# Cross attention on one core: x1 and x2 stored by halves of n, and the first batch's keys and scores made in two halves of m

## Chip, cores and metric

The kernel runs on one core of a Trainium2 chip. The metric is the device time of one execution in microseconds, given as the median of several runs. The kernel before takes 717.22 us (three runs, 717.07 to 717.47).

## What is computed

```python
# B, C1, C2, N = 8, 512, 512, 1024; D = 64; float32
q = jnp.einsum('bcn,dc->bnd', x1, Wq) + bq
k = jnp.einsum('bcn,dc->bdn', x2, Wk) + bk[:, None]
v = jnp.einsum('bcn,dc->bdn', x2, Wv) + bv[:, None]
attn = jax.nn.softmax(jnp.einsum('bnd,bdm->bnm', q, k), axis=2)
attn_out = jnp.einsum('bcm,bnm->bcn', v, attn)
return attn_out + x1
```

For each of eight batches, x1 (512 channels by 1024 positions n) gives queries and x2 (512 by 1024 positions m) gives keys and values. The softmax runs over m.

## The kernel before, in words

Everything is float32. The kernel never forms v: it computes y = x2 times the exponentials, transposed, divides by their sum, and then takes Wv times y, plus bv, plus x1. Both of these products are cut into 2 by 2 blocks and done with seven block products instead of eight; sums of blocks on the left (`left_sums`, L91: S1 to S4) and on the right (`right_sums`, L233: T1 to T4) are made by DVE (VectorE). `MULT` (L259) lists the seven products with their operands and the PSUM banks, "a" or "c", that collect them. In the text "product 6" is entry 6 of this table. `first(i)` (L435) is one of the products with x2, `second(i)` (L438) one of those with Wv.

**A batch** has two halves of n, h = 0 and 1, of 512. The scores are laid with m on the partitions: eight blocks of 128 values of m, by 512 of n. `scores` (L164) makes a pair of such blocks, i of 0 to 3, g of 0 and 1: two matmuls, one on the upper and one on the lower 64 rows of TensorE (PE). In the kernel before, pair i holds m block i (g = 0) and block 4 + i (g = 1), and lies in the tile `e[h]` at `[:, :, i, :]`. `fold` (L194) takes the running maximum (later the sum) over pairs on DVE, `highest` (L207) folds the two g and lets POOL (GpSimd) reduce over partitions to `top`. `exponentials` (L227) subtracts `top` on DVE and takes exp on ACT (ScalarE). `total` and `shares` do the same for the sums and their reciprocals.

**Projections.** `project` (L130) makes q or k of a whole batch: for each of four channel blocks c, one matmul of 64 columns for n below 512 into PSUM partitions 0 to 63 and one for n from 512 into partitions 64 to 127, each with 512 columns to stream. `load_x` (L111) loads x1 or x2 of a batch in four transfers of 512 KB, one per channel block, into one tile `x` that has a single buffer: x2 of a batch is issued when the queries have read x1 of it, and x1 of the next batch when the keys have read x2.

**Order.** The order of each engine's instructions is the order in which the program issues them (`manual_schedule`); a framework adds the waits. Each engine takes its instructions strictly in that order. Loads and stores are issued from one queue, SP's; ACT's queue issues the weights wqk and a copy of q's halves to the other partitions (L156). When ACT copies a score pair that DVE also reads from PSUM, it waits for DVE's reading.

**The head** (L349) is batch 0 up to its first product. SP issues, in this order: x1 for h = 0 in two transfers of two channel blocks each (rows of 2 KB), x2 in four transfers (rows of 4 KB), a11 (a transposed block of x2), x1 for h = 1 in two, a21, a22, a12, and the four blocks of Wv. PE does ten warm-up matmuls, then q of h = 0 on both partition halves (`head_queries`, L339, bank c1), k of all m (bank c0), four score pairs (two in the double-buffered "sc" banks, one in a0 and a1, one in c0 and c1), q of h = 1 in bank a0, three score pairs of h = 1, and then `first(1)`, the first product, whose right operand is the exponentials of g = 0. ACT copies the score pairs to SBUF in the order 0, 2, 3, 1. DVE folds pair 1 from PSUM and pairs 2 and 3 from the copies, and makes S1 and S2 of batch 0 while POOL reduces the maximum.

**`head_second`** (L408) follows in period 0 (`period`, L431), after `first(1)`: the fourth score pair of h = 1, the queries of batch 1, the second half's maximum, S3 and S4 of batch 0, and the exponentials of h = 1. Then come `sum_e(T1, T2)`, which makes the right operand of product 6, and, on PE, `first(2)`, the keys of batch 1 and `first(6)`.

**The end of period 0.** DVE adds bias and x1 to what the banks hold (`evict_o`, L319): the results 11, 22, 12 and 21 in this order. Before 12, it makes S1 to S4 of batch 1 (L529). Result 12 is in bank a, which `first(1)` of batch 1 opens anew. Each eviction issues its stores on SP; `fetch_o` (L312) loads x1 again for it.

The order of the first copies and folds is set in these lines (L386 to L392):

```python
        copies = [scores(s, 0, i, bank) for i, bank in enumerate((None, None, "a", "c"))]
        copies[0]()
        fold(s, 0, 1, "max", ALU.max, copies[1].ps)
        for i in (2, 3, 1):
            copies[i]()
        fold(s, 0, 2, "max", ALU.max)
        fold(s, 0, 3, "max", ALU.max)
```

Of the kernel before, what the change touches and what calls it, by code (L numbers as in the profile page):

```python
# [15 lines left out]
def kernel(  # L16
# [39 lines left out]

    nc = tc.nc
    P = 128
    B, C, N = x1.shape
    D = wqk.shape[3]  # L60
    CT = C // P
    H = 512
# [41 lines left out]
    class Batch:  # L104
        def __init__(self, b):
# [2 lines left out]
            self.mx, self.top, self.den, self.rden = {}, {}, {}, {}  # L108
            self.tmp, self.bank = {}, {}

    def load_x(s, x):  # L111

        s.x = sb.tile([P, CT, N], F32, tag="x", name=f"x_{s.b}_{x.tensor.name}")
        for c in range(CT):
            nc.sync.dma_start(s.x[:, c, :], x[s.b, ts(c, P), :])

    def load_a(s, *ks):
        for k in ks:
# [8 lines left out]
                s.a[k] = sb.tile([P, MH, C // 2], F32, tag=f"a{k}", name=f"a{k}_{s.b}")  # L127
        left_sums(s.a, *ks)

    def project(s, nm, w_sb, bank=None):  # L130

        if bank:
            ps = ps_a.tile([P, H], F32, tag=bank, name=f"ps_{nm}_{s.b}")
        else:
            ps = ps_s.tile([P, 2, H], F32, tag="sc", name=f"ps_{nm}_{s.b}")[:, 0, :]
        for c in range(CT):
            for h, r in ((0, lo), (1, hi)):
                nc.tensor.matmul(  # L138
                    ps[r, :],
                    w_sb[:, c, :],  # L140
                    s.x[:, c, ts(h, H)],
                    start=(c == 0),
                    stop=(c == CT - 1),
                )
        return ps
# [9 lines left out]
        for h, r, o in ((0, lo, hi), (1, hi, lo)):  # L155
            nc.scalar.dma_start(s.q[o, ts(h, H)], s.q[r, ts(h, H)])  # L156

    def keys(s, bank=None):

        ps = project(s, "k", wk_sb, bank)  # L160
        s.k = sb.tile([P, H], F32, tag="k", name=f"k_{s.b}", bufs=2)
        nc.scalar.activation(s.k, ps, AF.Identity, bias=bk_sb)

    def scores(s, h, i, bank=None):  # L164


        if i == 0:
            s.e[h] = sb.tile([P, 2, MH, H], F32, tag=f"e{h}", name=f"e_{s.b}_{h}")
        e = s.e[h]
        if bank:  # L170
            whole = None
            ps = [
                ps_a.tile([P, H], F32, tag=f"{bank}{g}", name=f"ps_s{bank}{g}_{s.b}_{h}_{i}")
                for g in range(2)
            ]
        else:
            whole = ps_s.tile([P, 2, H], F32, tag="sc", name=f"ps_s_{s.b}_{h}_{i}")
            ps = [whole[:, g, :] for g in range(2)]
        for g, r in ((0, lo), (1, hi)):
            nc.tensor.matmul(  # L180
                ps[g], s.k[r, ts(i, P)], s.q[r, ts(h, H)], start=True, stop=True
            )

        def copy():
            if bank:
                for g in range(2):
                    nc.scalar.copy(e[:, g, i, :], ps[g])  # L187
            else:
                nc.scalar.copy(e[:, :, i, :], whole)  # L189

        copy.ps = whole
        return copy

    def fold(s, h, i, kind, op, ps=None):  # L194

        e = s.e[h]
        if i == 1:
            s.mx[h] = sb.tile([P, 2, H], F32, tag="fold", name=f"{kind}_{s.b}_{h}", bufs=2)
        f = s.mx[h]
        new = e[:, :, i, :] if ps is None else ps  # L200
        nc.vector.tensor_tensor(f, e[:, :, 0, :] if i == 1 else f, new, op)  # L201

    def fold_halves(s, h, op):
        f = s.mx[h]
# [20 lines left out]
        nc.scalar.activation(e, e, AF.Exp)  # L225

    def exponentials(s, h, i):  # L227
        e = s.e[h][:, :, i, :]
        top = s.top[h].unsqueeze(1).to_broadcast([P, 2, H])
        nc.vector.tensor_tensor(e, e, top, ALU.subtract)  # L230
        nc.scalar.activation(e, e, AF.Exp)  # L231
# [80 lines left out]
    def fetch_o(s, k):  # L312

        for j in range(2):
            c, h = 2 * (int(k[0]) - 1) + j, int(k[1]) - 1
            s.o[k, j] = sb.tile([P, H], F32, tag="o", name=f"o{k}{j}_{s.b}", bufs=6)
            nc.sync.dma_start(s.o[k, j], x1[s.b, ts(c, P), ts(h, H)])

    def evict_o(s, k):  # L319
        bank, add = RESULT[k]  # L320
# [18 lines left out]
    def head_queries(s, x_sb, h, bank):  # L339

        ps = ps_a.tile([P, H], F32, tag=bank, name=f"ps_q_{s.b}_{h}")
        for c in range(CT):
            for r in (lo, hi):
                nc.tensor.matmul(
                    ps[r, :], wq_sb[:, c, :], x_sb[:, c, ts(h, H)], start=(c == 0), stop=(c == CT - 1)
                )
        nc.scalar.activation(s.q[:, ts(h, H)], ps, AF.Identity, bias=bq_sb)  # L347

    def head(s):  # L349

        s.q = sb.tile([P, N], F32, tag="q", name=f"q_{s.b}", bufs=2)
        x1_sb = sb.tile([P, CT, N], F32, tag="x", name="x1_head")
        x2_sb = sb.tile([P, 2, MH, H], F32, tag="e1", name="x2_head")
        s.x = x2_sb.rearrange("p a (b t) n -> p (a b) (t n)", t=2)

        def load_x1(c, h):  # L360
            nc.sync.dma_start(
                x1_sb[:, c : c + 2, ts(h, H)],
                x1[s.b, c * P : (c + 2) * P, ts(h, H)].rearrange("(t p) n -> p t n", p=P),
            )

        nc.gpsimd.dma_start(bqk_sb, bqk)
        nc.gpsimd.dma_start(bv_sb, bv)
        nc.scalar.dma_start(wqk_sb, wqk)
        warm = const.tile([P, P], F32, name="warm")
        nc.vector.memset(warm, 0.0)  # L370
        ps = ps_a.tile([P, H], F32, tag="a0", name="ps_warm")
        for _ in range(WARM):
            nc.tensor.matmul(ps[:, 0:P], warm, warm, start=True, stop=True)
        load_x1(0, 0)
        load_x1(2, 0)
        for c in range(CT):
            nc.sync.dma_start(s.x[:, c, :], x2[s.b, ts(c, P), :])
        nc.scalar.activation(warm[:, 0:1], warm[:, 0:1], AF.Exp)
        load_a(s, "11")
        load_x1(0, 1)  # L380
        load_x1(2, 1)
        load_a(s, "21", "22", "12")
        load_values()
        head_queries(s, x1_sb, 0, "c1")
        keys(s, "c0")
        copies = [scores(s, 0, i, bank) for i, bank in enumerate((None, None, "a", "c"))]  # L386
        copies[0]()
        fold(s, 0, 1, "max", ALU.max, copies[1].ps)
        for i in (2, 3, 1):
            copies[i]()  # L390
        fold(s, 0, 2, "max", ALU.max)
        fold(s, 0, 3, "max", ALU.max)  # L392
        highest(s, 0)
        sum_a(s, "S1", "S2")
        head_queries(s, x1_sb, 1, "a0")
        load_x(states[1], x1)
        copies = [scores(s, 1, 0), scores(s, 1, 1), scores(s, 1, 2, "c")]
        for g in range(2):
            for i in range(MH):
                first_exponentials(s, g, i)  # L400
        for copy in copies:
            copy()
        fold(s, 0, 1, "sum", ALU.add)
        fold(s, 0, 2, "sum", ALU.add)
        fold(s, 1, 1, "max", ALU.max)
        fold(s, 0, 3, "sum", ALU.add)

    def head_second(s, n):  # L408
# [5 lines left out]
        queries(n)  # L414
        load_x(n, x2)
        highest(s, 1)
        sum_a(s, "S3", "S4")
        for i in range(MH):
            exponentials(s, 1, i)

# [10 lines left out]
    def period(s, n, nn, nnn):  # L431
# [94 lines left out]
        second(7)  # L526
        evict_o(s, "22")
        if s.b == 0:
            sum_a(n, "S1", "S2", "S3", "S4")  # L529
        if n:  # L530
            second(3)
            evict_o(s, "12")
            second(4)
            evict_o(s, "21")
        else:
            second(4)
            evict_o(s, "21")
# [39 lines left out]
```

## Time and profile before

| | |
|---|---|
| median of the runs | 717.22 us |
| the profiled execution's own time | 716.93 us |
| its span, first to last instruction | 714.9 us |
| PE busy | 705.6 us (99%), 1892 instructions |
| weight loads (PEld) busy | 299.8 us (42%) |
| DVE busy | 590.2 us (83%), 569 instructions |
| ACT busy | 201.3 us (28%) |
| POOL busy | 97.2 us (14%) |
| DMA | 87.39 MB, mean 122 GB/s |
| granted TensorE clock | 1.000 of full speed |

Busy time is the time in which an engine executes instructions, waiting left out; the 2.0 us between the execution's own time and its span lie before the first and after the last instruction. A line of the timeline gives start and duration in us, engine, source line, operation, output and inputs by the names of their tiles, sizes and the number of instructions that it merges. What stands in brackets is how long the engine was idle ahead of it, and what released it. Matmuls are pipelined, so that a row's duration reaches some tenths beyond the start of the next. One float32 matmul of the program is two rows of the profile. The tile names `ps_ya` and `ps_yc` are the banks a and c in the products with x2, `ps_oa` and `ps_oc` those with Wv, `ps_s`, `ps_sa`, `ps_sc` are scores in the "sc", a and c banks, `aS` and `a` are blocks of x2 and their sums, `eT` the sums of exponentials.

### The profile page before, as it was taken

Reading aid. Unit: us, or ns where it says so; the run is one execution under the profiler, and the core shown is the slowest. Engines: PE = TensorE matmul, PEld = TensorE weight load, DVE = VectorE, ACT = ScalarE, POOL = GpSimd, SP = SyncE. Lnnn points to the kernel's source line nnn. Section 1 sums busy time; section 2 is a strip of 40 time slices with the busy share of each in tenths; the row PEclk is TensorE's granted clock in tenths of the full one; section 3 lists DMA queues with packets and bytes.
Section 4 is the critical chain, followed back from the end, with each engine's and each line's share of the span. In section 5 each row is a group of like instructions: output and inputs, shape, how many; then the busy total and the mean of one; then the engine's idle time right before and its main releaser. Section 6 shows DMA issues by size and latency. Waiting matters only on the chain.

```text
span 714.9 us, 5407 instructions
## 1 busy us (share of the span) xinstructions
PE 705.6 (99%) x1892; PEld 299.8 (42%) x1892; DVE 590.2 (83%) x569; ACT 201.3 (28%) x271; POOL 97.2 (14%) x38
## 2 busy tenths in 40 slices
PE   8999999999999999999999999999999999999997
PEld 4333444434444434444344444443434444444443
DVE  0999899988979888798887987889887898989454
ACT  2733412043211522224231232403324034220010
POOL 0132030030200211021200202002020020301000
PEclk9999999999999999999999999999999999999999
DMA  8577132441333503435133252232601350042004
GB/s 333 210 235 256 68 147 101 156 154 46 147 146 119 189 8 141 148 118 191 58 119 127 109 191 98 108 118 89 220 0 61 117 177 0 0 161 75 0 1 147
DMA packets 34699, 87.39 MB, mean 122 GB/s; under 512 B 3952, under 2 KB 3952, under 8 KB 34672
## 3 DMA queue, kind: packets, MB, share of 16 engines
q1 hardware_dynamic: 33344, 84.95, 33.6%
q10 hardware_dynamic: 1264, 2.10, 0.9%
q8 instruction: 15, 0.25, 0.1%
q14 instruction: 12, 0.10, 0.0%
q0 software_dynamic: 64, 0.00, 0.0%
HBM read 68.42 MB, written 16.78 MB: 119 GB/s over the span
## 4 chain that ended last, share of the span: by engine, by line
PE 87%; DVE 8%; DMA 1%; issue 1%; ACT 1%; SPq 0%; POOL 0%; DVEq 0%; ACTq 0%; POOLq 0%
PE ps_ya L279 27%; PE ps_yc L279 21%; PE ps_oa L279 15%; PE ps_oc L279 11%; PE ps_s L180 5%; PE ps_k L138 3%; PE ps_q L138 3%; DVE max L201 1%; DMA x_head<-in_x_dram 1%; DVE eT L236 1%; DVE e L230 1%; DVE aS L100 1%; PE ps_sa L180 1%; DVE den L219 1%; PE ps_sc L180 1%
## 5 line engine op out<-in xcount | busy, mean ns | idle before, releaser
L215 POOL PARTITION_ALL_REDUCE den<-sum x16 | 65.3, 4081 | 433.2 <-DVE sum L205 433.2
L279 PE MATMUL ps_ya<-eT,aS 128*128 128x512 f32 x256 | 113.1, 595 | 0.0
L279 PE MATMUL ps_yc<-e,a 128*128 128x512 f32 x256 | 112.6, 592 | 0.0
L289 ACT COPY uy<-ps_ya 128x512 f32<-128x512 f32 x48 | 28.1, 588 | 233.2 <-PE ps_ya L279 233.2
L230 DVE TENSOR_TENSOR e<-e,top 128x1024 f32<-128x1024 f32 x60 | 70.0, 1219 | 13.9 <-POOL top L210 13.9
L279 PEld LDWEIGHTS ps_ya<-eT,aS 128*128 128x128 f32 x256 | 48.0, 190 | 63.8 <-issue 63.6
L279 PEld LDWEIGHTS ps_yc<-e,a 128*128 128x128 f32 x256 | 48.6, 190 | 61.6 <-issue 60.1
L324 DVE SCALAR_TENSOR_TENSOR o<-ps_oc,bv_sb,o 128x512 f32<-128x512 f32 x48 | 35.7, 749 | 41.6 <-PE ps_oc L279 41.5
L231 ACT ACTIVATE e<-e 128x1024 f32<-128x1024 f32 x60 | 62.2, 1056 | 22.2 <-DVE e L230 20.4
L289 ACT COPY uo<-ps_oa 128x512 f32<-128x512 f32 x48 | 28.1, 586 | 132.4 <-PE ps_oa L279 131.1
L189 ACT COPY e<-ps_s 128x1024 f32<-128x1024 f32 x47 | 46.7, 1027 | 61.5 <-PE ps_s L180 61.5
L279 PE MATMUL ps_ya<-e,a 128*128 128x512 f32 x128 | 56.4, 594 | 1.3 <-ACT e L225 0.8
L279 PE MATMUL ps_oc<-y,w 128*128 128x512 f32 x128 | 57.5, 592 | 0.0
L279 PE MATMUL ps_oa<-yT,w_S 128*128 128x512 f32 x128 | 57.5, 592 | 0.0
L279 PE MATMUL ps_yc<-eT,a 128*128 128x512 f32 x128 | 57.0, 598 | 0.0
L279 PE MATMUL ps_ya<-e,aS 128*128 128x512 f32 x128 | 56.2, 592 | 0.0
L219 DVE RECIPROCAL den<-den 128x512 f32<-128x512 f32 x16 | 53.6, 3349 | 0.0
L180 PE MATMUL ps_s<-q,k 64*128 64x512 f32 x188 | 47.9, 608 | 1.6 <-ACT q L347 0.8
L210 POOL PARTITION_ALL_REDUCE top<-max x16 | 30.3, 1897 | 131.3 <-DVE max L205 131.3
L308 DVE TENSOR_TENSOR y<-ps_yc,uy 128x512 f32<-128x512 f32 x48 | 31.2, 676 | 15.0 <-PE ps_yc L279 14.9
L201 DVE TENSOR_TENSOR max<-max,e 128x1024 f32<-128x1024 f32 x32 | 39.2, 1225 | 3.7 <-ACT e L187 0.5
L201 DVE TENSOR_TENSOR sum<-sum,e 128x1024 f32<-128x1024 f32 x32 | 39.2, 1225 | 2.1
(65 smaller groups left out, 757.5 us busy)
## 6 DMA issues: line engine op xcount, KB each, us to landing
x_in_x_dram<-in_x_dram SPq DMA_DIRECT2D x56, 512.0 KB, 5.4
a<-in_x2T_dram SPq DMA_DIRECT2D x32, 512.0 KB, 4.2
o<-in_x_dram SPq DMA_DIRECT2D x64, 256.0 KB, 6.4
out_dram<-o SPq DMA_DIRECT2D x64, 256.0 KB, 2.1
x_head<-in_x_dram SPq DMA_DIRECT2D x8, 512.0 KB, 8.0
q<-q ACTq DMA_DIRECT2D x14, 128.0 KB, 6.9
w<-in_wvT_dram SPq DMA_DIRECT2D x4, 256.0 KB, 8.9
wqk_sb<-in_wqk_dram ACTq DMA_DIRECT2D x1, 256.0 KB, 4.7
```

The source lines that it names most:

```text
L138: nc.tensor.matmul(ps[r, :], w_sb[:, c, :], s.x[:, c, ts(h, H)], start=(c == 0), stop=(c == CT - 1),)
L180: nc.tensor.matmul(ps[g], s.k[r, ts(i, P)], s.q[r, ts(h, H)], start=True, stop=True)
L189: nc.scalar.copy(e[:, :, i, :], whole)
L201: nc.vector.tensor_tensor(f, e[:, :, 0, :] if i == 1 else f, new, op)
L215: nc.gpsimd.partition_all_reduce(s.den[h], s.mx[h][:, 0, :], P, ReduceOp.add)
L219: nc.vector.reciprocal(s.rden[h], s.den[h])
L230: nc.vector.tensor_tensor(e, e, top, ALU.subtract)
L231: nc.scalar.activation(e, e, AF.Exp)
L279: nc.tensor.matmul(ps, left[ka][:, k, ts(j, P)], right[kb][:, k, :], start=opens and k == 0, stop=i in (2, 3, 4) and k == n_k - 1, skip_gr ...
L289: nc.scalar.copy(s.tmp[i, j], ps)
L308: nc.vector.tensor_tensor(y[:, j, :], ps, s.tmp[add, j], ALU.add)
L324: nc.vector.scalar_tensor_tensor(o, s.bank[bank, j], bv_sb[:, c : c + 1], o, ALU.add, ALU.add)
```

## The change

The arrays x1 and x2 are stored in another order ahead of the launch: [batch, half of n, partition, channel block, 512], so that the values of one partition for one half lie together, two channel blocks in one row of 4 KB. All loads of x follow: `load_x` still has four transfers of 512 KB, but each holds two channel blocks of one half of n, in the order (c 0 and 1, h 0), (c 0 and 1, h 1), (c 2 and 3, h 0), (c 2 and 3, h 1).

In the head, SP issues x1 of h = 0, then x2 of the first half of m, then x2 of the second half, two transfers each; the rest stays in order. A new function `head_keys` projects half of the keys with matmuls of 256 columns: the first quarter of that half into partitions 0 to 63 and the second into 64 to 127. Pairs 0 and 1 now hold blocks of the first half of m, pairs 2 and 3 of the second; `pair` finds their places in `e[h]` for batch 0. PE's order in the head becomes: q of h = 0, first half of k (bank c0), pairs 0 and 1, second half of k (bank a0), pair 2 (c0, c1), pair 3 (a0, a1), q of h = 1 (bank c0). DVE folds pairs 2 and 3 from PSUM as well, in two instructions each, and each copy by ACT comes after the fold of its pair, in the order 0, 1, 2, 3, with the second half's k between copies 0 and 1.

S2 of batch 0 moves from the head to `head_second`, ahead of S3 and S4. S3 and S4 of batch 1 move from before `evict_o(12)` to after `evict_o(21)`.

```diff
@@ -56,7 +56,7 @@
 
     nc = tc.nc
     P = 128
-    B, C, N = x1.shape
+    B, C, N = out.shape
     D = wqk.shape[3]
     CT = C // P
     H = 512
@@ -108,11 +108,18 @@
             self.mx, self.top, self.den, self.rden = {}, {}, {}, {}
             self.tmp, self.bank = {}, {}
 
+        def pair(self, h, i):
+
+            if self.b:
+                return self.e[h][:, :, i, :]
+            return self.e[h][:, i // 2, i % 2 :: 2, :]
+
     def load_x(s, x):
 
-        s.x = sb.tile([P, CT, N], F32, tag="x", name=f"x_{s.b}_{x.tensor.name}")
-        for c in range(CT):
-            nc.sync.dma_start(s.x[:, c, :], x[s.b, ts(c, P), :])
+        s.x = sb.tile([P, 2, CT, H], F32, tag="x", name=f"x_{s.b}_{x.tensor.name}")
+        for c in range(0, CT, 2):
+            for h in range(2):
+                nc.sync.dma_start(s.x[:, h, c : c + 2, :], x[s.b, h, :, c : c + 2, :])
 
     def load_a(s, *ks):
         for k in ks:
@@ -127,18 +134,15 @@
                 s.a[k] = sb.tile([P, MH, C // 2], F32, tag=f"a{k}", name=f"a{k}_{s.b}")
         left_sums(s.a, *ks)
 
-    def project(s, nm, w_sb, bank=None):
-
-        if bank:
-            ps = ps_a.tile([P, H], F32, tag=bank, name=f"ps_{nm}_{s.b}")
-        else:
-            ps = ps_s.tile([P, 2, H], F32, tag="sc", name=f"ps_{nm}_{s.b}")[:, 0, :]
+    def project(s, nm, w_sb):
+
+        ps = ps_s.tile([P, 2, H], F32, tag="sc", name=f"ps_{nm}_{s.b}")[:, 0, :]
         for c in range(CT):
             for h, r in ((0, lo), (1, hi)):
                 nc.tensor.matmul(
                     ps[r, :],
                     w_sb[:, c, :],
-                    s.x[:, c, ts(h, H)],
+                    s.x[:, h, c, :],
                     start=(c == 0),
                     stop=(c == CT - 1),
                 )
@@ -155,9 +159,9 @@
         for h, r, o in ((0, lo, hi), (1, hi, lo)):
             nc.scalar.dma_start(s.q[o, ts(h, H)], s.q[r, ts(h, H)])
 
-    def keys(s, bank=None):
-
-        ps = project(s, "k", wk_sb, bank)
+    def keys(s):
+
+        ps = project(s, "k", wk_sb)
         s.k = sb.tile([P, H], F32, tag="k", name=f"k_{s.b}", bufs=2)
         nc.scalar.activation(s.k, ps, AF.Identity, bias=bk_sb)
 
@@ -166,9 +170,8 @@
 
         if i == 0:
             s.e[h] = sb.tile([P, 2, MH, H], F32, tag=f"e{h}", name=f"e_{s.b}_{h}")
-        e = s.e[h]
+        e = s.pair(h, i)
         if bank:
-            whole = None
             ps = [
                 ps_a.tile([P, H], F32, tag=f"{bank}{g}", name=f"ps_s{bank}{g}_{s.b}_{h}_{i}")
                 for g in range(2)
@@ -184,21 +187,24 @@
         def copy():
             if bank:
                 for g in range(2):
-                    nc.scalar.copy(e[:, g, i, :], ps[g])
+                    nc.scalar.copy(e[:, g, :], ps[g])
             else:
-                nc.scalar.copy(e[:, :, i, :], whole)
-
-        copy.ps = whole
+                nc.scalar.copy(e, whole)
+
+        copy.ps = ps if bank else whole
         return copy
 
     def fold(s, h, i, kind, op, ps=None):
 
-        e = s.e[h]
         if i == 1:
             s.mx[h] = sb.tile([P, 2, H], F32, tag="fold", name=f"{kind}_{s.b}_{h}", bufs=2)
         f = s.mx[h]
-        new = e[:, :, i, :] if ps is None else ps
-        nc.vector.tensor_tensor(f, e[:, :, 0, :] if i == 1 else f, new, op)
+        if isinstance(ps, list):
+            for g in range(2):
+                nc.vector.tensor_tensor(f[:, g, :], f[:, g, :], ps[g], op)
+        else:
+            new = s.pair(h, i) if ps is None else ps
+            nc.vector.tensor_tensor(f, s.pair(h, 0) if i == 1 else f, new, op)
 
     def fold_halves(s, h, op):
         f = s.mx[h]
@@ -225,7 +231,7 @@
         nc.scalar.activation(e, e, AF.Exp)
 
     def exponentials(s, h, i):
-        e = s.e[h][:, :, i, :]
+        e = s.pair(h, i)
         top = s.top[h].unsqueeze(1).to_broadcast([P, 2, H])
         nc.vector.tensor_tensor(e, e, top, ALU.subtract)
         nc.scalar.activation(e, e, AF.Exp)
@@ -314,7 +320,7 @@
         for j in range(2):
             c, h = 2 * (int(k[0]) - 1) + j, int(k[1]) - 1
             s.o[k, j] = sb.tile([P, H], F32, tag="o", name=f"o{k}{j}_{s.b}", bufs=6)
-            nc.sync.dma_start(s.o[k, j], x1[s.b, ts(c, P), ts(h, H)])
+            nc.sync.dma_start(s.o[k, j], x1[s.b, h, :, c, :])
 
     def evict_o(s, k):
         bank, add = RESULT[k]
@@ -342,26 +348,39 @@
         for c in range(CT):
             for r in (lo, hi):
                 nc.tensor.matmul(
-                    ps[r, :], wq_sb[:, c, :], x_sb[:, c, ts(h, H)], start=(c == 0), stop=(c == CT - 1)
+                    ps[r, :], wq_sb[:, c, :], x_sb[:, h, c, :], start=(c == 0), stop=(c == CT - 1)
                 )
         nc.scalar.activation(s.q[:, ts(h, H)], ps, AF.Identity, bias=bq_sb)
 
+    def head_keys(s, x_sb, h, bank):
+
+        ps = ps_a.tile([P, H // 2], F32, tag=bank, name=f"ps_k_{s.b}_{h}")
+        for c in range(CT):
+            for g, r in ((0, lo), (1, hi)):
+                nc.tensor.matmul(
+                    ps[r, :],
+                    wk_sb[:, c, :],
+                    x_sb[:, h, c, ts(g, H // 2)],
+                    start=(c == 0),
+                    stop=(c == CT - 1),
+                )
+        nc.scalar.activation(s.k[:, ts(h, H // 2)], ps, AF.Identity, bias=bk_sb)
+
     def head(s):
 
 
 
 
 
+
         s.q = sb.tile([P, N], F32, tag="q", name=f"q_{s.b}", bufs=2)
-        x1_sb = sb.tile([P, CT, N], F32, tag="x", name="x1_head")
+        s.k = sb.tile([P, H], F32, tag="k", name=f"k_{s.b}", bufs=2)
+        x1_sb = sb.tile([P, 2, CT, H], F32, tag="x", name="x1_head")
         x2_sb = sb.tile([P, 2, MH, H], F32, tag="e1", name="x2_head")
-        s.x = x2_sb.rearrange("p a (b t) n -> p (a b) (t n)", t=2)
-
-        def load_x1(c, h):
-            nc.sync.dma_start(
-                x1_sb[:, c : c + 2, ts(h, H)],
-                x1[s.b, c * P : (c + 2) * P, ts(h, H)].rearrange("(t p) n -> p t n", p=P),
-            )
+
+        def load(x_sb, x, h):
+            for c in range(0, CT, 2):
+                nc.sync.dma_start(x_sb[:, h, c : c + 2, :], x[s.b, h, :, c : c + 2, :])
 
         nc.gpsimd.dma_start(bqk_sb, bqk)
         nc.gpsimd.dma_start(bv_sb, bv)
@@ -371,28 +390,26 @@
         ps = ps_a.tile([P, H], F32, tag="a0", name="ps_warm")
         for _ in range(WARM):
             nc.tensor.matmul(ps[:, 0:P], warm, warm, start=True, stop=True)
-        load_x1(0, 0)
-        load_x1(2, 0)
-        for c in range(CT):
-            nc.sync.dma_start(s.x[:, c, :], x2[s.b, ts(c, P), :])
+        load(x1_sb, x1, 0)
+        load(x2_sb, x2, 0)
+        load(x2_sb, x2, 1)
         nc.scalar.activation(warm[:, 0:1], warm[:, 0:1], AF.Exp)
         load_a(s, "11")
-        load_x1(0, 1)
-        load_x1(2, 1)
+        load(x1_sb, x1, 1)
         load_a(s, "21", "22", "12")
         load_values()
         head_queries(s, x1_sb, 0, "c1")
-        keys(s, "c0")
-        copies = [scores(s, 0, i, bank) for i, bank in enumerate((None, None, "a", "c"))]
+        head_keys(s, x2_sb, 0, "c0")
+        copies = [scores(s, 0, 0), scores(s, 0, 1)]
         copies[0]()
-        fold(s, 0, 1, "max", ALU.max, copies[1].ps)
-        for i in (2, 3, 1):
+        head_keys(s, x2_sb, 1, "a0")
+        copies += [scores(s, 0, 2, "c"), scores(s, 0, 3, "a")]
+        for i in range(1, MH):
+            fold(s, 0, i, "max", ALU.max, copies[i].ps)
             copies[i]()
-        fold(s, 0, 2, "max", ALU.max)
-        fold(s, 0, 3, "max", ALU.max)
         highest(s, 0)
-        sum_a(s, "S1", "S2")
-        head_queries(s, x1_sb, 1, "a0")
+        sum_a(s, "S1")
+        head_queries(s, x1_sb, 1, "c0")
         load_x(states[1], x1)
         copies = [scores(s, 1, 0), scores(s, 1, 1), scores(s, 1, 2, "c")]
         for g in range(2):
@@ -414,7 +431,7 @@
         queries(n)
         load_x(n, x2)
         highest(s, 1)
-        sum_a(s, "S3", "S4")
+        sum_a(s, "S2", "S3", "S4")
         for i in range(MH):
             exponentials(s, 1, i)
 
@@ -526,12 +543,14 @@
         second(7)
         evict_o(s, "22")
         if s.b == 0:
-            sum_a(n, "S1", "S2", "S3", "S4")
+            sum_a(n, "S1", "S2")
         if n:
             second(3)
             evict_o(s, "12")
             second(4)
             evict_o(s, "21")
+            if s.b == 0:
+                sum_a(n, "S3", "S4")
         else:
             second(4)
             evict_o(s, "21")
@@ -555,8 +574,8 @@
     from concourse.bass_utils import run_bass_kernel_spmd as _run
 
     laid = {
-        "x1": _np.asarray(x),
-        "x2": _np.asarray(ctx_2048),
+        "x1": _np.asarray(x).reshape(8, 4, 128, 2, 512).transpose(0, 3, 2, 1, 4),
+        "x2": _np.asarray(ctx_2048).reshape(8, 4, 128, 2, 512).transpose(0, 3, 2, 1, 4),
         "x2T": _np.asarray(ctx_2048).reshape(8, 2, 256, 2, 4, 128).transpose(0, 1, 3, 5, 4, 2),
         "wqk": _np.stack([_np.asarray(L0_xattn_Wq), _np.asarray(L0_xattn_Wk)]).reshape(2, 64, 4, 128).transpose(3, 0, 2, 1),
         "bqk": _np.stack([_np.asarray(L0_xattn_bq), _np.asarray(L0_xattn_bk)] * 2).reshape(2, 2, 64).transpose(0, 2, 1).reshape(128, 2),
```

## The prediction, made before the result was known

> **What bounds the kernel now.** First the busy table by stretches: it tells where TensorE (PE) is not busy at all. Columns: stretch, its length, then busy us (count) of PE, weight loads, DVE, ACT, POOL, clock, DMA share, GB/s.
>
> ```profile
> 6.00:14.36 8.36, 7.35 (x32) 2.29 (x33) 0.00 (x0) 1.37 (x2) 0.00 (x0) 1.00 1.03 401
> 14.36:26.12 11.76, 10.14 (x45) 3.60 (x45) 8.83 (x9) 5.36 (x9) 2.68 (x1) 1.00 0.98 365
> 26.12:50.00 23.88, 23.88 (x71) 8.91 (x72) 23.52 (x24) 15.16 (x21) 2.69 (x1) 1.00 0.49 161
> 50.00:126.00 76.00, 75.30 (x204) 31.40 (x203) 71.52 (x71) 24.09 (x31) 15.08 (x5) 1.00 0.43 155
> 126.00:700.00 574.00, 574.00 (x1500) 245.00 (x1499) 479.47 (x458) 153.25 (x206) 75.19 (x25) 1.00 0.30 106
> ```
>
> From 126 us on PE never stops; before, it loses time only in the head (to 26.12) and twice in batch 0. The change can act there alone, plus whatever it adds to PE later. The list of PE's waits names the two late ones, in place of which the timeline of PE has these rows (start, duration):
>
> ```profile
> 1.04 4.41 PE L373 MATMUL ps_warm<-warm 128*128 128x128 f32 x20 [1.04 <-DVE warm L370]
> ...
> 9.48 2.81 PE L138 MATMUL ps_k<-x_head,wqk_sb 128*64 128x512 f32 x12
> 12.49 1.08 PE L138 MATMUL ps_k<-x_head,wqk_sb 128*64 128x512 f32 x4 [0.20 <-DMA x_head<-in_x_dram]
> 14.36 1.99 PE L180 MATMUL ps_s<-q,k 64*128 64x512 f32 x8 [0.79 <-ACT k L162]
> 17.99 3.65 PE L344 MATMUL ps_q<-x_head,wqk_sb 128*64 128x512 f32 x16
> 22.44 1.99 PE L180 MATMUL ps_s<-q,k 64*128 64x512 f32 x8 [0.79 <-ACT q L347]
> 26.12 7.13 PE L279 MATMUL ps_ya<-e,a 128*128 128x512 f32 x16 [0.83 <-ACT e L225]
> ...
> 85.95 1.29 PE L180 MATMUL ps_sa<-q,k 64*128 64x512 f32 x3 [0.20 <-DVE y L306]
> ...
> 123.72 2.84 PE L279 MATMUL ps_ya<-e,a 128*128 128x512 f32 x6 [0.51 <-DVE o L324]
> ```
>
> The head ends where the first product starts, 26.12. What ends last there is the exponential (0.83 of wait); PE itself was free at about 25.2 (last score at 24.69, 0.43, a change of shape 0.1). So an earlier maximum is worth at most 0.9 unless PE comes earlier too. Projections and scores take 0.43 per "slot" (two 512-column passes, a pair of column or row halves side by side): 16 rows of q in 3.44.
>
> The timeline around 38 to 48 us shows two things that are close in batch 0: DVE sums beside a POOL reduction, and batch 1's keys waiting for the last of x2.
>
> ```profile
> 37.53 1.22 DVE L100 TENSOR_TENSOR a<-a,a 128x1024 f32<-128x1024 f32 x1
> 37.71 2.69 POOL L210 PARTITION_ALL_REDUCE top<-max  x1 [13.30 <-DVE max L205]
> 38.67 2.06 DVE L100 TENSOR_TENSOR aS<-a,aS 128x1024 f32<-128x1024 f32 x1
> 40.65 4.62 DVE L230 TENSOR_TENSOR e<-e,top 128x1024 f32<-128x1024 f32 x4
> 46.37 0.43 PEld L138 LDWEIGHTS ps_k<-x_in_x_dram,wqk_sb 128*64 128x64 f32 x4 [0.43 <-DMA x_in_x_dram<-in_x_dram]
> 47.67 0.20 PEld L138 LDWEIGHTS ps_k<-x_in_x_dram,wqk_sb 128*64 128x64 f32 x4 [0.87 <-DMA x_in_x_dram<-in_x_dram]
> ```
>
> **What the Trainium skill says.** (1) "TensorE: Matmul & The Clock Gate", Back-to-back issue gap: 262 cycles for 256 columns, 518 for 512, so a narrow slot is half a wide one. No 256-column matmul is in this trace; 512 columns take 0.43 per slot. (2) "SBUF — State Buffer", Who interferes with whom: a DVE instruction with two SBUF inputs and a GpSimd instruction that reads SBUF exclude each other. The trace agrees: the second sum above took 2.06 instead of 1.22, and the reduction ran 2.69 there but only 1.78 at 76.45, beside no DVE work. (3) "DMA: Bandwidth & Descriptors", Queues, rings and completion order: an engine takes a queue's descriptors in ring order. The trace agrees: the loads of one queue land in the order of issue.
>
> **The change, part by part.** Times are on the axis of the profiled execution: span 714.9, own time 716.93 (2.0 outside), 0.3 below the median of 717.22.
>
> *Loads of the head.* Same eight transfers, same order, but x1 in 4 KB instead of 2 KB rows. Between PE's two waits for x1 at 5.99 and 7.49 lie 1.50 for 512 KB; x2 in 4 KB rows takes 1.28 (11.21 to 12.49). The second x1 transfer is needed only at 7.75, so only the first counts, and it shares the engines with wqk. I take -0.1 (bounds -0.25, +0.1, since rows now lie 8 KB apart).
>
> *Keys in halves.* k's first half needs only the queue's third and fourth transfers; both are in before PE has finished q (9.48). Eight narrow slots of an estimated 0.215 (skill's ratio on the 0.43 row): last starts at 10.99. A wide last slot started 0.64 before ACT; less 0.21 for half the columns: ACT at 11.41. A 128x512 k took 0.69; ACT's slope from 128x512 to 128x1024 is 0.43 (0.63, 1.06), so 128x256 costs 0.47: done 11.88, first scores at 11.94, against 14.36. **2.4 gained here.** Four score slots (1.82 as at 14.36 to 16.18), 0.1 for the change of shape, eight narrow slots: the second half's last slot starts at 15.42, its data long there (12.49). ACT 15.84 to 16.31, scores of pairs 2 and 3 from 16.36. So PE waits for ACT twice, where it waited once: 0.7 more (15.63 to 16.36).
>
> *Folds from PSUM.* Pair 2 reaches DVE 1.17 later (14.36 to 15.54), at 17.53. Four 128x512 folds 0.60 apart, last 0.68 (the y<-ps_yc row: two in 1.28): end 20.0; halves to 20.74 (0.69); then S1, and POOL ends 1.64 after S1 as before (22.76 to 24.40): 23.5. Without S2, DVE starts e at once; 0.68 and ACT 0.63: first exponential at 25.0, 1.1 earlier than 26.06.
>
> *What is late next.* q's second half moved from bank a0 to c0, which pair 2 uses. It has to wait for fold c0 (to 18.2) and then ACT's copy of c0 (0.60, to 18.85; behind it on ACT are three more copies and q, done by 20.7, in time for q's 22.6): q starts at 18.9, against 17.99. Behind it in PE's queue are all of half 1's scores and the first product. From q's start to PE's first free slot are 7.2 (17.99 to 25.2): **26.1. The product starts where it did (26.12)**, bound by PE instead of the exponential. Head: 0.0, with the loads -0.1.
>
> *S2 moved behind the second maximum.* Three sums instead of two stand between it and the exponentials. Half 1's third copy is bound by PE's score at 33.18, so the maximum comes only 0.25 earlier (DVE no longer late at 34.34): halves 36.7 to 37.4, S2 to 38.5, S3 blocked until POOL's end (38.5+1.64=40.1) plus the 0.33 seen at 40.73: 40.5, S4 to 41.6. The exponentials start 0.9 later than 40.65. DVE then has no gap up to 76 and hands its lateness on to the eviction L306 that holds PE at 85.95. **+0.9** (0.0 if S3 isn't blocked; 1.2 if the 0.25 isn't won).
>
> *load_x by pairs of c and halves of n.* Channel block 2 now needs the last transfer, not the third. Batch 1's keys would read it at 46.66; it lands just before 47.67 (row above). Blocks 2 and 3, four slots, start at 47.67 instead of two: **+0.86** on PE (bounds 0 and 1.5: the landing moves with the copies of q on the same engines by some 0.7). The other twelve such projections have their x in 2 us or more before (next least: q at 59.38, last x issued at 50.11 and landed at 57.0): nothing. The last two parts run side by side: PE is 0.86 late, DVE 0.9, and PE meets DVE at 85.95. Together **+0.9**, not 1.8.
>
> *S3 and S4 of batch 1 moved behind evict_o 12 and 21.* Two DVE sums (1.22 each) leave the queue ahead of L324, for which PE waits at 123.72. With 2.4 less, that eviction ends at 122.1, before PE asks at 123.15: **-0.57** (0.67 of gap less 0.1 for the shape). DVE is 0.7 late behind it, but had 3.2 idle at 169 to 173. Stores of o go out earlier or 2 us later; nobody waits for them.
>
> *At nothing:* fetch_o's new pitch (same 2 KB rows) and pair()'s strides (DVE and ACT rows keep their size), all covered by PE; were the fetches late, PE would wait at an eviction for each us.
>
> Sum: -0.1 + 0.9 - 0.57 = **+0.2**; profiled 717.1, median 717.5.
>
> **Rivals.** *Narrow slots cost as much as wide ones* (weight loads, not columns, set the pace of head_keys): two chains of seven slots at 0.215 more are 3.0 on PE's path: 720.5, slower. For it: a narrow slot loads as many weights as a wide one. Against: the warm-up's twenty 128-column loads with their matmuls took 4.41, 0.22 each, and a narrow slot loads two times 64 columns. It decides (+1.43 in all) from a slot of 0.30. *The late costs don't arrive:* x2's last block lands by 46.7, and S3 isn't blocked. Then -0.1-0.57: 716.6. For it: the copies of q that share the DMA engines at 42 to 46 could shift; against: two equal blockings of a second sum. *The 2.4 is kept,* if q's second half weren't held by c0: exponential 25.0 would count only with PE at 25.2, -0.9 more: 716.6 with the late costs. Against: the bank's two readers stand in the code.
>
> **Chances.** The forecast (716.9 to 718.2) 0.58; late costs absent 0.11; gain kept 0.07; both, 715.6, 0.04; narrow slots dear 0.16 (0.02 of it within 0.2%, 0.04 below 719.0); an unnamed cost 0.04. Range 716.4 to 719.0, which holds 0.80. The measurement can tell about 0.2%, 1.43 us, from no change: faster 0.04, same 0.58+0.11+0.07+0.02 = 0.78, slower 0.18.
>
> **What would show it.** First scores near 11.9; two k projections of 1.7 to 1.9; q's second half near 18.9 waiting for ACT's copy; first product near 26.0 with no wait for ACT e; batch 1's keys stopping at block 2 for about 1.0; the first e<-e,top of half 1 near 41.5; the wait at 123.7 gone. I am wrong if narrow rows stand 0.3 or more apart, if the product starts before 25.5, or if a later projection waits for x.

## The result, and the profile after

The changed kernel takes 717.61 us (median of 12 runs, 717.34 to 719.51); the kernel before took 717.21 beside it (12 runs, 717.07 to 717.47). The ratio is 1.001, with a 95% interval of 1.0001 to 1.0019: slower by 0.1 to 1.4 us, at the edge of what this measurement can tell. The forecast was 717.5. The profiled execution of the changed kernel took 717.58, its span is 715.6 (before: 716.93 and 714.9).

First the table by stretches, as the prediction read it for the kernel before (stretch, length, busy us and count of PE, weight loads, DVE, ACT, POOL, then clock, DMA share, GB/s). This is the changed kernel:

```profile
6.00:14.36 8.36, 7.79 (x40) 2.81 (x41) 0.00 (x0) 1.90 (x3) 0.00 (x0) 1.00 1.02 383
14.36:26.12 11.76, 9.86 (x54) 3.88 (x52) 7.59 (x11) 5.94 (x11) 2.68 (x1) 1.00 0.83 311
26.12:50.00 23.88, 23.15 (x70) 8.28 (x67) 22.66 (x22) 13.98 (x19) 2.69 (x1) 1.00 0.58 187
50.00:126.00 76.00, 76.00 (x208) 32.26 (x206) 70.94 (x71) 24.48 (x32) 15.07 (x5) 1.00 0.46 156
126.00:700.00 574.00, 574.00 (x1500) 244.99 (x1499) 481.35 (x460) 153.21 (x206) 75.15 (x25) 1.00 0.31 105
```

After 126 us nothing has changed: PE is busy throughout, as before. Ahead of it, PE idles in a new place (0.73 between 26 and 50 us) and no longer between 50 and 126 (0.70 before). Idle time alone doesn't balance, though: over the first four rows it fell by 0.13 us (3.33 to 3.20), while the span grew by 0.7. The rest sits in rows that count as busy but run stretched, so from here on the reading goes by the starts of rows. PE's timeline in the head:

```profile
5.91 4.11 PE L350 MATMUL ps_q<-x_head,wqk_sb 128*64 128x512 f32 x16 [0.23 <-DMA wqk_sb<-in_wqk_dram]
9.86 2.01 PE L360 MATMUL ps_k<-x_head,wqk_sb 128*64 128x256 f32 x16
12.44 1.99 PE L183 MATMUL ps_s<-q,k 64*128 64x512 f32 x8 [0.57 <-ACT k L367]
14.36 1.95 PE L360 MATMUL ps_k<-x_head,wqk_sb 128*64 128x256 f32 x16
16.88 1.13 PE L183 MATMUL ps_sc<-q,k 64*128 64x512 f32 x4 [0.57 <-ACT k L367]
...
19.40 3.65 PE L350 MATMUL ps_q<-x_head,wqk_sb 128*64 128x512 f32 x16 [0.53 <-ACT e L190]
23.84 1.99 PE L183 MATMUL ps_s<-q,k 64*128 64x512 f32 x8 [0.79 <-ACT q L353]
...
26.62 3.70 PE L285 MATMUL ps_ya<-e,a 128*128 128x512 f32 x8
```

The predicted order is there, some 0.5 later from the first rows on: two k projections of 2.0 and 1.95, q's second half held by ACT's copy, and a first product that no longer waits for an exponential. The first q row lasts 4.11 where it lasted 3.65, for the same sixteen instructions: one slot at its start ran at about half pace. The trace's record of the TensorE clock reaches full speed at 6.87 us here, after q's start at 5.91; before, it did so at 5.07, ahead of q's start at 6.03. Of the eight experiments below, with the same q ahead, two show such a row (4.18 and 4.00; record at 7.19 and 6.72, q from 6.09 and 5.98) and six show 3.65 (record at 4.3 to 5.8, ahead of q's start in each). So this 0.46 goes with the moment at which the clock's record turns full, which differs between executions, and is no part of the change. From q's start to the product, less this 0.46, are 20.25; before they were 20.09.

The stretch in which the head's lateness grows is at the keys of batch 1. First the kernel before, then the changed one:

```profile
44.89 3.87 PE L138 MATMUL ps_k<-x_in_x_dram,wqk_sb 128*64 128x512 f32 x16
48.68 7.13 PE L279 MATMUL ps_ya<-eT,aS 128*128 128x512 f32 x16
```

```profile
45.39 1.94 PE L142 MATMUL ps_k<-x_in_x_dram,wqk_sb 128*64 128x512 f32 x8
47.85 1.07 PE L142 MATMUL ps_k<-x_in_x_dram,wqk_sb 128*64 128x512 f32 x2 [0.52 <-DMA x_in_x_dram<-in_x_dram]
49.13 1.93 PE L142 MATMUL ps_k<-x_in_x_dram,wqk_sb 128*64 128x512 f32 x6 [0.22 <-DMA x_in_x_dram<-in_x_dram]
51.00 3.27 PE L285 MATMUL ps_ya<-eT,aS 128*128 128x512 f32 x7
```

PE stops twice: ahead of block 2, as predicted, and again within it, for the other half of n. The product behind them started at 48.68 before; it is 2.32 late, 0.50 of it from the head, 1.82 from here. In what follows, the stop of the keys is the time from their first row to the product behind them, less the 3.79 that the kernel before took (44.89 to 48.68). The DVE rows of the same stretch:

```profile
37.77 1.22 DVE L100 TENSOR_TENSOR aS<-aS,a 128x1024 f32<-128x1024 f32 x1
38.91 2.06 DVE L100 TENSOR_TENSOR a<-a,a 128x1024 f32<-128x1024 f32 x1
40.89 1.21 DVE L100 TENSOR_TENSOR aS<-a,aS 128x1024 f32<-128x1024 f32 x1
42.03 2.35 DVE L236 TENSOR_TENSOR e<-e,top 128x1024 f32<-128x1024 f32 x2
```

Three sums instead of two stand ahead of the exponentials, again with the second one stretched to 2.06 (POOL's reduction runs from 37.95 for 2.69), and the exponentials start 1.38 later than 40.65: 0.50 from the head, 0.88 from the sum. Last, PE's rows at the scores near 86 us (where PE waited before) and at the product of batch 1:

```profile
86.08 1.99 PE L183 MATMUL ps_s<-q,k 64*128 64x512 f32 x8
87.90 1.21 PE L183 MATMUL ps_sa<-q,k 64*128 64x512 f32 x4
88.75 1.21 PE L183 MATMUL ps_s<-q,k 64*128 64x512 f32 x4
89.90 1.51 PE L142 MATMUL ps_k<-x_in_x_dram,wqk_sb 128*64 128x512 f32 x6
...
124.49 4.03 PE L285 MATMUL ps_ya<-e,a 128*128 128x512 f32 x9
```

Neither has a wait. Here is what the bracketed 0.20 of the kernel before amounted to:

```profile
83.76 1.99 PE L180 MATMUL ps_s<-q,k 64*128 64x512 f32 x8
...
86.91 0.59 PE L180 MATMUL ps_s<-q,k 64*128 64x512 f32 x1
87.08 0.59 PE L180 MATMUL ps_sa<-q,k 64*128 64x512 f32 x1
...
88.46 2.80 PE L138 MATMUL ps_k<-x_in_x_dram,wqk_sb 128*64 128x512 f32 x12
```

From the first score to the next projection it took 4.70 us; the changed kernel takes 3.82 for the same matmuls. So PE, 2.32 late at 86, is only 1.44 late at k. The wait for result 12 at 123 is gone and takes back 0.67 by the starts (1.44 late at k, 0.77 late at 124.49) and 0.1 in the first row behind it: 1.44 - 0.78 = 0.66, the growth of the span (714.90 to 715.56).

### The profile page after: what moved, and what is told of

The parts are those of the page before. It is cut to its first block, busy times and chain, and to the rows that moved or that the text cites. A ratio compares the mean times of both kernels' runs of the same rounds, so it can differ in the third digit from the quotient of the medians.

```text
span 715.6 us, 5444 instructions
## 1 busy us (share of the span) xinstructions
PE 706.7 (99%) x1908; PEld 301.3 (42%) x1908; DVE 589.4 (82%) x571; ACT 201.6 (28%) x272; POOL 97.2 (14%) x38
## 4 chain that ended last, share of the span: by engine, by line
PE 97%; DMA 2%; ACT 0%; DVE 0%; SPq 0%; issue 0%
PE ps_ya L285 31%; PE ps_yc L285 22%; PE ps_oa L285 15%; PE ps_oc L285 12%; PE ps_s L183 6%; PE ps_q L142 4%; PE ps_k L142 3%; DMA x_in_x_dram<-in_x_dram 1%; PE ps_sc L183 1%; PE ps_q L350 1%; PE ps_sa L183 1%; DMA wqk_sb<-in_wqk_dram 1%; PE ps_k L360 1%; SPq L122 0%; ACT k L367 0%; DVE o L330 0%
## 5 line engine op out<-in xcount | busy, mean ns | idle before, releaser
L207 DVE TENSOR_TENSOR max<-max,e 128x1024 f32<-128x1024 f32 x30 | 36.8, 1225 | 4.2 <-ACT e L192 0.9
```

The costliest lines, as they stand in the source:

```text
L207: nc.vector.tensor_tensor(f, s.pair(h, 0) if i == 1 else f, new, op)
```

## The theory, its rivals, and a table that separates them

Theory: the change does three things that count, late in batch 0 and not in the head: (1) x2's later landing holds the keys for 1.82; (2) S2 makes DVE late at the eviction near 86, where PE meets it, so that of (1), less the wait that PE had there anyway, and (2) the larger counts and not the sum; (3) S3 and S4 out of the way give 0.78 back near 124. Rivals: A, the keys alone make the kernel late (load rows as before, and 716.7 follows); B, the two add up; C, DVE alone counts (S2 back in the head helps by itself). And for the head: the 2.4 that the first scores win is given back at q's bank; the rival is that it is lost elsewhere.

Each kernel's profiled execution splits at two rows of PE: the first product (`ps_ya<-e,a`), and the k projection that follows the scores near 86. What lies ahead of the first row holds the head with its clock; between them lie (1) and (2); behind them (3).

| kernel | first product | that k | between | from k to the span's end | median of runs |
|---|---|---|---|---|---|
| before | 26.12 | 88.46 | 62.34 | 626.4 | 717.21 |
| after | 26.62 | 89.90 | 63.28 | 625.7 | 717.61 |
| keys' x by blocks again | 26.05 | 89.33 | 63.28 | 625.7 | 717.41 |
| S2 in the head again | 26.30 | 89.72 | 63.42 | 625.7 | 717.85 |
| both | 26.75 | 88.89 | 62.14 | 625.7 | 716.33 |
| x in whole pieces of 512 KB | 26.14 | 89.43 | 63.29 | 625.7 | 717.36 |
| q of h = 1 in another bank | 25.91 | 89.56 | 63.65 | 625.7 | 716.95 |
| both, S3 and S4 back | 26.46 | 88.60 | 62.14 | 626.4 | 716.75 |
| both, and q's bank | 25.56 | 87.70 | 62.14 | 625.7 | 715.43 |
| the same, evictions swapped | 25.68 | 86.88 | 61.20 | 625.7 | 714.71 |

The times behind k fall into two values: each kernel that has S3 and S4 ahead of result 12 has 626.4, each other one 625.7. All experiments are edits of the changed kernel, timed beside the kernel before (median 717.17 in both groups of runs).

## The experiments

**The keys' x by channel blocks again.** Batches 1 to 7 load x as the kernel before did, from copies of x1 and x2 in the old order; the head keeps the new one. The diff shows the loads; the index of `project` and the callers follow.

```diff
-        s.x = sb.tile([P, 2, CT, H], F32, tag="x", name=f"x_{s.b}_{x.tensor.name}")
-        for c in range(0, CT, 2):
-            for h in range(2):
-                nc.sync.dma_start(s.x[:, h, c : c + 2, :], x[s.b, h, :, c : c + 2, :])
+        s.x = sb.tile([P, CT, N], F32, tag="x", name=f"x_{s.b}_{x.tensor.name}")
+        for c in range(CT):
+            nc.sync.dma_start(s.x[:, c, :], x[s.b, ts(c, P), :])
```

> The changed kernel, but batches 1 to 7 load x1 and x2 as before, one channel block of 1024 positions per transfer, from copies in the old layout; the head keeps halves. Theory (two late costs side by side: keys waiting for x2 on PE, S2 behind the second maximum on DVE, joined at the eviction before the second scores of batch 1): batch 1's keys no longer stop (under 0.3 us instead of 1.07), but DVE is as late as in the changed kernel, PE waits again for the eviction from bank a at about 86, and the time stays at 717.6 (717.3 to 717.9). Rival A (the wait of the keys is the whole cost, DVE's lateness is covered): 716.7. Rival B (the costs add up on PE): 715.8.

Measured: 717.41, ratio 1.0004 (0.9996 to 1.0012). The keys' stop shrinks to 0.3, and PE's timeline of this kernel shows where that goes:

```profile
84.36 1.99 PE L184 MATMUL ps_s<-q,k 64*128 64x512 f32 x8
86.83 1.29 PE L184 MATMUL ps_sa<-q,k 64*128 64x512 f32 x3 [0.48 <-DVE y L313]
```

PE arrives 1.7 earlier, 0.6 of it from the head, and waits for the eviction instead. Between the two rows lie 63.28, exactly as in the changed kernel. A falls: taking away the larger stop alone brings nothing.

**S2 in the head again.**

```diff
-        sum_a(s, "S1")
+        sum_a(s, "S1", "S2")
...
-        sum_a(s, "S2", "S3", "S4")
+        sum_a(s, "S3", "S4")
```

> The changed kernel with S2 of batch 0 back in the head, beside S1. Theory: DVE's subtractions of the second half start some 1.1 us earlier (about 41 instead of 42.0), the keys of batch 1 still stop for about 1.1 us, PE doesn't wait at the eviction, and the time stays at 717.6 (717.3 to 717.9). Rival A (only the keys' wait costs): 717.6 too. Rival C (DVE's lateness is the whole cost): 716.7.

Measured: 717.85, ratio 1.0009 (1.0001 to 1.0018). DVE starts the exponentials of h = 1 at 40.58, and no wait is left near 86; the keys still stop, for 2.14 (45.08 to 51.01). PE's timeline of this kernel:

```profile
48.20 2.88 PE L142 MATMUL ps_k<-x_in_x_dram,wqk_sb 128*64 128x512 f32 x8 [0.83 <-DMA x_in_x_dram<-in_x_dram]
51.01 3.27 PE L285 MATMUL ps_ya<-eT,aS 128*128 128x512 f32 x7
```

63.42 between the rows: C falls too. Over the kernel before, S2 alone (the first experiment) costs 0.94 and the keys alone (this one) 1.08.

**Both.** The two edits together.

> Both edits at once: loads of batches 1 to 7 by channel block from the old layout, and S2 back in the head. Theory: only now does the cost go, 0.9 us: 716.7 (716.4 to 717.0), and PE waits at the eviction at about 86 as the kernel before did. Rivals A and C: no more than their own single edit gave. Rival B: 715.8 or less.

Measured: 716.33 (21 runs), ratio 0.9988 (0.9982 to 0.9995), a little below the expected 716.4 to 717.0; 62.14 between the rows, 1.14 less than in the changed kernel. Singly the edits gave 0.00 and -0.14. That is what a meeting of two late engines looks like, and B falls: added up, 0.94 and 1.08 would be 2.0 in the changed kernel, which has 0.94. That the stretch of "both" stands 0.20 below that of the kernel before fits the maximum won in the head: DVE's exponentials of h = 1 start 14.28 after the product (41.03 and 26.75), before 14.53.

**x in whole pieces of 512 KB.** x is stored so that each transfer of `load_x` and of the head reads one contiguous piece. The transfers hold the same values in the same order; only the distance between rows, 8 KB in the changed kernel, goes. The diff shows `load_x`; the head's loads and `fetch_o` follow in the same way.

```diff
-                nc.sync.dma_start(s.x[:, h, c : c + 2, :], x[s.b, h, :, c : c + 2, :])
+                nc.sync.dma_start(s.x[:, h, c : c + 2, :], x[s.b, c // 2, h])
```

> The changed kernel with x1 and x2 stored so that each 512 KB transfer is one contiguous block (rows of 4 KB next to each other, not 8 KB apart); order, sizes and sums as in the changed kernel. If the pitch of 8 KB is what made the loads of batch 1 slow: the first transfer of x2 lands 3.2 us after its issue instead of 4.3, the last 9.7 after the first issue instead of 10.7, the keys stop for 0.3 us in all instead of 1.07, the third transfer of the head lands 1.3 after the second instead of 2.2. The time stays near 717.5, since DVE is still late (717.2 to 717.8). If the pitch is not the reason, the landings stay as in the changed kernel.

Measured: 717.36, ratio 1.0001 (0.9992 to 1.0009). The last line of the answer on x's tile tells how long the four x2 transfers of batch 1 take from issue to landing (shortest, median, longest). In the kernel before:

```profile
DMA to landing us min/median/max: 3.2/6.4/8.4
```

In the changed kernel:

```profile
DMA to landing us min/median/max: 4.3/7.5/9.3
```

In this experiment:

```profile
DMA to landing us min/median/max: 3.5/6.7/8.5
```

With the pitch go 0.8 of the 0.9 to 1.1 us. PE's timeline of this kernel at the keys:

```profile
44.91 4.81 PE L142 MATMUL ps_k<-x_in_x_dram,wqk_sb 128*64 128x512 f32 x16
49.65 2.84 PE L285 MATMUL ps_ya<-eT,aS 128*128 128x512 f32 x6
```

The keys' stop falls from 1.82 to 0.95, about half, and not to the expected 0.3. The x2 of this experiment lands like that of the first one (3.4, 6.8 and 8.7 there), which has the old grouping of the transfers and a stop of 0.3. So about half of the 1.82 is the pitch, and most of the rest is the new grouping, which the prediction priced at 0.86. To PE the gain is worth nothing, for the same reason as in the first experiment (63.29 between the rows). In the head the expectation failed: the third transfer of the queue still lands 2.7 after the second (2.2 in the changed kernel), and k's first half still waits for x2 (0.19 in the bracket). In the seven other experiments, whose head loads are those of the changed kernel, the same transfer lands 1.4 to 1.7 after the second; so the 2.2 differs between executions too, and its cause stays open.

**q of h = 1 in another bank.** A test of the head: q's second half goes into a free "sc" bank, so that it has no fold and no copy to wait for.

```diff
-        head_queries(s, x1_sb, 1, "c0")
+        head_queries(s, x1_sb, 1)
...
+            ps = ps_s.tile([P, 2, H], F32, tag="sc", name=f"ps_q_{s.b}_{h}")[:, 0, :]
```

> The changed kernel with one edit in the head: q of the second half of n goes to a free double-buffered score bank instead of c0, so that it has no fold and no copy to wait for. Theory (the head's 2.4 us are given back at the bank c0): q starts 0.6 us earlier, right behind the fourth score pair, the first product starts 0.6 earlier and is still bound by PE, all later stages of batch 0 follow, and the time falls from 717.6 to 717.0 (716.7 to 717.3). Rival D (the head isn't on the path, since loads or DVE bind in batch 0): 717.6.

Measured: 716.95, ratio 0.9996 (0.9988 to 1.0004). PE's timeline:

```profile
18.70 3.65 PE L353 MATMUL ps_q<-x_head,wqk_sb 128*64 128x512 f32 x16
23.14 1.99 PE L183 MATMUL ps_s<-q,k 64*128 64x512 f32 x8 [0.79 <-ACT q L356]
...
25.91 1.55 PE L285 MATMUL ps_ya<-e,a 128*128 128x512 f32 x3
```

The wait at q is gone and the head is 0.6 shorter (19.53 from first q to product, where the experiments that keep its order and loads have 20.1 to 20.2, the stretched slot left out). The bank was a limit, as the prediction said, but worth 0.6, not 2.4: the rival is right for the larger part. The rest was never to be had. PE's listed waits from q's start to the product summed to 2.61 before (0.20, 0.79, 0.79, 0.83) and to 2.46 in the changed kernel (0.57, 0.57, 0.53, 0.79), where 0.11 for x2 sit unlisted in the first row of k besides (2.01, in the first experiment 1.90); PE had the same products to make, only in another order. In its row of the table this kernel loses 0.37 again between the product and k (63.65, after 63.28): PE comes to the keys 0.70 earlier, but x2 lets their last rows start only 0.14 earlier (48.99, after 49.13). Of the 0.66 between the medians of the two kernels, these 0.6 and 0.37 explain 0.2; the rest stays open.

**Both, with S3 and S4 of batch 1 back before result 12.**

```diff
-            sum_a(n, "S1", "S2")
+            sum_a(n, "S1", "S2", "S3", "S4")
...
-            if s.b == 0:
-                sum_a(n, "S3", "S4")
```

> The head's change alone: keys and scores in halves, folds from PSUM, halves layout in the head. Loads of batches 1 to 7 by channel block from the old layout, S2 back in the head, S3 and S4 of batch 1 back before the eviction of 12. Theory: the head by itself gives nothing, so the time is that of the kernel before, 717.2 (716.9 to 717.5), 0.8 above the kernel that only keeps the moved S3 and S4 (716.3), and PE waits for the eviction at about 123.7 again. Rival E (the head gains, and the moved S3 and S4 gain nothing): 716.3.

Measured: 716.75, ratio 0.9995 (0.9987 to 1.0003), below the expected 716.9 to 717.5. The wait of the kernel before is back:

```profile
123.86 4.56 PE L286 MATMUL ps_ya<-e,a 128*128 128x512 f32 x10 [0.51 <-DVE o L331]
```

Behind k lie 626.4 again instead of 625.7: the move is worth 0.8 in the trace. Between the medians of this kernel and of "both" lie only 0.42, less than the trace says; the intervals of their ratios overlap, and what makes the rest of the difference stays open.

**Both, and q's bank; and then the evictions in another order.** Two combinations, to see whether the parts hold together. The second one also lets DVE free bank a first in batch 0: `evict_y(12)`, which frees it, goes ahead of the second step of `evict_y(22)`, the multiplication by the reciprocals.

```diff
-        evict_y(s, "22")
+        evict_y(s, "22", (1, 2) if s.b else (1,))
         first(3)
         evict_y(s, "12")
+        if s.b == 0:
+            evict_y(s, "22", (2,))
```

> The kernel with both late costs taken back (loads of batches 1 to 7 by channel block, S2 in the head; 716.3) and q of the second half of n in a score bank. Theory: the 0.6 us of the bank come on top: 715.7 (715.4 to 716.1). Rival D: 716.3.

> As the kernel before it in this list, and in batch 0 DVE evicts result 12 from bank a ahead of the second step of result 22 (two multiplications by the reciprocals). Theory: the wait of PE for bank a at about 85 with its split pairs of scores costs 0.7 to 0.9 us, not the 0.2 that the profile puts in brackets; two instructions of 0.6 us less ahead of the eviction take it away: 715.0 (714.7 to 715.4). Rival F (only the 0.2 in brackets is lost): 715.5.

Measured: 715.43, ratio 0.9978 (0.9969 to 0.9987), and 714.71 (5 runs), ratio 0.9967 (0.9954 to 0.9979), 2.5 us below the kernel before. The first keeps "both"'s 62.14 and adds the 0.6 of q's bank (again 19.53 from first q to product). In it PE shows no wait near 86 at all, and still the rows split:

```profile
83.27 1.99 PE L184 MATMUL ps_s<-q,k 64*128 64x512 f32 x8
...
86.15 0.59 PE L184 MATMUL ps_s<-q,k 64*128 64x512 f32 x1
86.32 0.59 PE L184 MATMUL ps_sa<-q,k 64*128 64x512 f32 x1
...
87.70 3.65 PE L143 MATMUL ps_k<-x_in_x2n_dram,wqk_sb 128*64 128x512 f32 x16
```

With the evictions swapped:

```profile
83.24 1.99 PE L184 MATMUL ps_s<-q,k 64*128 64x512 f32 x8
85.06 1.02 PE L184 MATMUL ps_sa<-q,k 64*128 64x512 f32 x4
85.92 1.02 PE L184 MATMUL ps_s<-q,k 64*128 64x512 f32 x4
86.88 3.65 PE L143 MATMUL ps_k<-x_in_x2n_dram,wqk_sb 128*64 128x512 f32 x16
```

From first score to k are 4.43 in the first, 3.64 in the second: 0.8 for a wait that the first lists nowhere, and the rival that expected only the bracketed 0.2 of the swap falls. The two banks of a pair come free 0.6 apart (two evictions in 1.28), and while only one is free, its matmul runs without its partner on the other half of the rows. In the kernel before, with 4.70, the same place cost 1.06, not the 0.20 in the bracket.

## Why the prediction was right

The forecast of 717.5 stands 0.1 below the median, and the predicted sum of +0.2 against +0.4 between the medians. Its mechanisms were right step by step, but two sizes were far off, and that they cancel is luck:

- *Loads of the head, -0.1:* q starts 0.12 earlier (5.91, before 6.03), but at 5.9 to 6.4 in the experiments with the same loads (5.4 with contiguous ones), so the term is within the scatter; the wait listed ahead of q is now for the weights wqk and not for x1. "Both are in before PE has finished q" was misread: in the kernel before, too, the fourth transfer lands only at 9.89, after 9.48. In the changed kernel it lands at 10.74, and k is held 0.11 for it.
- *Keys in halves, and the head, 0.0:* narrow slots took 0.214 to 0.216 (0.215 estimated), ACT's narrow k 0.47 (0.47). q's second half came at 19.40, which is 18.94 less the stretched slot (18.9 predicted). The head's net is +0.16 in this execution, 0.0 to 0.1 in the four experiments that keep its order and its loads. The rival of dear narrow slots is dead; "the 2.4 is kept" is too, and with the bank out of the way only 0.6 would have been.
- *S2, +0.9:* DVE's exponentials at 42.03 less 0.50 are 41.53 (41.5 predicted). Alone, with x by blocks, it costs 63.28 - 62.34 = 0.94.
- *Keys of batch 1, +0.86:* the place was right, the size was not. The step took the landing of the last x2 from the kernel before and allowed only the copies of q to move it. Rows of 4 KB at a pitch of 8 KB landed 0.9 to 1.1 later from their own issue, and the stop was 1.82, above the upper bound of 1.5. With contiguous rows it was 0.95, near what the step gave: it had left out the pitch.
- *Together +0.9, not 1.8:* measured 63.28 - 62.34 = 0.94, and shown by the first three experiments. The larger stop at the keys cost nothing more because PE's wait near 86, read as the bracketed 0.20, was worth 1.06: the keys alone would have cost 1.82 - 1.06 = 0.76, less than DVE's 0.94. The second experiment, where the keys alone are late, agrees: 2.14 - 1.06 = 1.08, as measured. That is the second wrong size, and it hid the first by luck. Had the wait been worth 0.20, this step would have come to 1.82 - 0.20 = 1.6.
- *S3 and S4, -0.57:* the wait is gone and 0.78 came back: the gap of 0.67, and 0.1 in the first row behind it (with the wait, ten rows take 4.56 there, in the first experiment, without it, 4.45). The step took 0.1 off the gap for the shape where 0.1 came on top.

In sum 0.16 + 0.46 - 0.12 for the head as executed, 0.94 and -0.78: +0.66, the growth of the span. Without the stretched slot it is +0.2, the forecast's sum. That the medians differ by 0.4 and not 0.2 is inside the interval of the ratio (0.1 to 1.4 us) and isn't explained further.

## What to carry to other kernels

On the engine that bounds a kernel, count the waits that a change takes out of it, not the time by which one step comes earlier: here the first scores came 2.3 earlier after q's start, and PE's listed waits in the head shrank by 0.15. Where two late engines meet, try both repairs together before dropping either: here each edit alone showed nothing. And measure a wait from start to start of the rows around it, against an undisturbed copy of the same rows: here the bracket held 0.20 of 1.06.

## What the runs showed of the hardware

- Loads of x2 of batch 1, 512 KB in 4 KB rows: the first took 4.3 to 4.8 us from issue to landing with rows 8 KB apart (three profiled executions), 3.2 to 3.6 when contiguous (seven).
- Two matmuls on the two row halves of TensorE, each with its own PSUM bank, ran side by side where both banks were free. Where one came free 0.6 us after the other, the pairs split and took 0.8 us longer (4.43 against 3.64), and no wait is listed.
- A TENSOR_TENSOR on DVE beside POOL's reduction: the first sum kept its 1.22, the second took 2.06, whichever sums they were (before, after and with S2 in the head). "SBUF — State Buffer", Who interferes with whom, in the Trainium skill says that they exclude each other; of the sums it is the second that pays here, and the reduction took 2.69, where it took 1.78 without DVE beside it (near 76 us in the kernel before).
- q's first row, after an equal warm-up, ran 0.4 to 0.5 longer in three of ten profiled executions: those in which it began before the clock's record reached full speed (6.7 to 7.2 us; 4.3 to 5.8 in the others).
